# Graph attention over 1,024 nodes: part of each query's edges kept in the query's row and added on GpSimd, the rest summed on TensorE, with a paced stream of projections

## The chip, the cores and the metric

One core of one Trainium2 chip. The time is device microseconds (us) of one execution of the whole program, inputs and outputs in HBM. The kernel before took 2595.01 us, the median of 3 runs (2594.36 to 2597.61).

## The reference, cut to what matters

Sixteen batches of 1,024 nodes with 512 features go through one layer of masked attention with 8 heads of 64, a residual and a layer norm. Everything is float32. The mask `adj` is the same for all batches and heads; it is sparse and uneven, since the chance of an edge falls with both node numbers.

```python
_w = (1.0 + jnp.arange(1024, dtype=jnp.float32)) ** -0.5
_w = _w / _w.mean()
_pij = jnp.clip(0.00390625 * _w[:, None] * _w[None, :], 0.0, 1.0)
adj = (jax.random.uniform(jax.random.fold_in(_gk, 2), (1024, 1024)) < _pij).astype(jnp.float32)
...
q = (x @ Wq + bq).reshape(b, n, H, HD)      # k and v alike
scores = jnp.einsum('bqhd,bkhd->bhqk', q, k) / jnp.sqrt(jnp.float32(HD))
scores = scores + (1.0 - adj)[None, None, :, :] * -1000000000.0
attn = jax.nn.softmax(scores, axis=-1)
out = jnp.einsum('bhqk,bkhd->bqhd', attn, v).reshape(b, n, d)
return _layernorm(x + out @ Wo + bo)
```

`adj` has 4,043 edges among 1,048,576 places. By tiles of 128 queries they are 1404, 588, 440, 377, 360, 311, 290 and 273; 60 queries have no edge, and their softmax is the mean over all keys.

## The kernel before, in words

The kernel works edge by edge. A *block* is 128 edges, one to a partition. `BLOCKS` gives how many blocks each of the eight query tiles has: 11, 6, 4, 4, 3, 3, 3, 3, in all 37 per batch and 592 for the 16 batches. During the lead-in `edges(t)` (line 271) reads the tile's rows of `adj`, finds the keys of each query with rounds of `max` (L286, L288) and writes for each block the list of key rows (`key_row`), of query rows (`query_row`) and a 128x128 matrix of zeros and ones (`sums`) that says which edge belongs to which query. Unused places of a block fetch row 0 and have a zero row in `sums`.

Projections (*fronts*): for each batch and each of its 8 tiles, `front` (line 393) gives 4 TensorE matmuls of 128x512 for q, for k and for v (L377), and a transposition of x two tiles ahead (L359). VectorE adds the biases (L397, L404), and the results go to HBM as rows: `q_rows` (512 wide) and `kv_rows` (1,024 wide, k and v side by side), each held for two batches. Row N of `kv_rows` has key zero and the mean of v, for a query without edges. Squares on ScalarE (L388) and sums on VectorE (L389) feed a guard: where the norms of q and k are too large for an exponential without a maximum, or the edges don't fit their blocks, a flag sends the work to `tile_general`.

Each block then goes through these operations:

- `gather`, 8 steps ahead: two indirect DMAs on GpSimd's queue, the query rows (L501, 128x512) and the key-value rows (L506, 128x1024)
- `scores`: on VectorE the product of query and key (L515, 128x512) and its sum by head (L517)
- `exponentials`: on ScalarE 128x8 (L522), written behind the weighted values in the tile `pv`
- `weigh`: v times the exponentials on VectorE (L533, 128x512). In batch 0 every second block, and in batch 15 two of three, are weighed on ScalarE with 8 operations (L529)
- `add_up`: two TensorE matmuls with `sums` as weights (L545, L546; each float32 matmul is two instructions) add the edges up by query, into PSUM, over the blocks of the tile

After the last block of a tile, `normalise` divides by the sum of exponentials on VectorE (L553, L554, L557), TensorE transposes (L566), and the tile is *done*. `finish` multiplies with Wo (L377, `po`), adds y, which is x loaded once more with the bias added on GpSimd (L461), and does the layer norm: L468, L471, L472, L474 on VectorE, L477 to L479 on GpSimd, L482 on ScalarE, and the store.

The order is written out by hand, one step `n` of the loop at line 594 per block, 34 lead-in steps ahead of block 0. A step issues the gather of block n+8, the weighing of block n+1, the scores of n+2, whatever earlier steps have put off to this one (`later`, collected in `plan`), the exponentials of n+2 and the sums of block n. Then TensorE gets units of projections and finishes until the step's `credit` is used up. `share`, the credit per step, is set once per batch from what is to be done (`PRODUCT` 0.86 a matmul, `TRANSPOSE` 0.44). Within a batch the fronts of the next batch come first, and the finishes only when no fronts are left. Each engine runs its instructions in this order. Tiles with a `tag` are rings of `bufs` buffers: who writes the next one waits until the last reader of the old one is through.

Of the kernel before, what the change touches and what calls it, by code (L numbers as in the profile page):

```python
# [9 lines left out]
F32 = mybir.dt.float32  # L10
# [123 lines left out]
def kernel(  # L134
# [29 lines left out]

    nc = tc.nc
# [7 lines left out]
    assert N == 1024 and D == 512 and HD == 64  # L173
    NB = sum(BLOCKS)
    first = [sum(BLOCKS[:t]) for t in range(NT)]

# [15 lines left out]
    with ExitStack() as main:  # L192
# [6 lines left out]
        def fill_psum(name):  # L199
            return psum.tile([P, HALF], F32, tag="fill", name=name, bufs=4)  # L200
# [7 lines left out]

        place = one.tile([P, max(BLOCKS) * P], F32, name="place")
        nc.gpsimd.iota(place, pattern=[[1, max(BLOCKS) * P]], base=1, channel_multiplier=0, allow_small_or_imprecise_dtypes=True)  # L210
# [15 lines left out]
        sums = one.tile([P, NB, P], F32, name="sums")  # L226
        key_row = one.tile([P, NB], I32, name="key_row")
        query_row = one.tile([P, NB], I32, name="query_row")
# [3 lines left out]
        kv_rows = [dram.tile([N + 1, 2 * D], F32, name=f"kv_rows_{i}") for i in range(2)]  # L232
        q_rows = [dram.tile([N, D], F32, name=f"q_rows_{i}") for i in range(2)]
        zero = one.tile([1, D], F32, name="zero")
        nc.gpsimd.memset(zero, 0.0)
        for i in range(2):
            nc.scalar.dma_start(kv_rows[i][N:N + 1, 0:D], zero)
# [7 lines left out]
        def bias_setup():  # L245
# [7 lines left out]
            bvb = work.tile([P, NPAIR, P], F32, tag="y", name="bvb", bufs=7)  # L253
# [17 lines left out]
        def edges(t):  # L271
            nb, J = BLOCKS[t], DEGREE[t]
# [5 lines left out]
            deg, end, lim, lone = (st[:, i:i + 1] for i in range(4))  # L278
            kl = small.tile([P, J + 2], F32, tag=f"kl{J}", name=f"kl_{t}", bufs=2)
            yield  # L280
# [4 lines left out]
            for r in range(J // 8):  # L285
# [7 lines left out]
            nc.vector.tensor_scalar(lone, kl[:, 0:1], 0.0, N + 1.0, op0=OP.is_le, op1=OP.mult)  # L293
            nc.vector.tensor_tensor(kl[:, 0:1], kl[:, 0:1], lone, op=OP.add)
            nc.vector.tensor_scalar(deg, deg, 1.0, None, op0=OP.max)
# [4 lines left out]
            nc.vector.tensor_copy(kl[:, J:J + 1], po[:, 0:1])  # L300
            nc.vector.tensor_copy(kl[:, J + 1:J + 2], query[:, t:t + 1])
            nc.vector.tensor_tensor(end, kl[:, J:J + 1], deg, op=OP.add)
            nc.vector.tensor_scalar(lim, end, -float(nb * P), 0.0, op0=OP.add, op1=OP.max)
            nc.vector.scalar_tensor_tensor(
                check[:, NT + t:NT + t + 1], deg, -float(J), lim, op0=OP.add, op1=OP.max
# [4 lines left out]
            nc.vector.tensor_scalar(o, span, kl[:, J:J + 1], None, op0=OP.is_gt)  # L310
# [3 lines left out]
            for i0 in range(0, nb, step):  # L314
# [16 lines left out]
                nc.vector.tensor_scalar(e[:, 1, :], e[:, 1, :], -1.0, 0.0, op0=OP.add, op1=OP.max)  # L331
                nc.vector.tensor_scalar(key_row[:, g0:g0 + n], e[:, 1, :], float(N), None, op0=OP.min)
# [60 lines left out]
        def front(b, t):  # L393

            def out_q(p):
                q = work.tile([P, D], F32, tag="q", name=f"q_{b}_{t}", bufs=2)
                nc.vector.scalar_tensor_tensor(q, p, scale, bq_bc, op0=OP.mult, op1=OP.add)  # L397
                nc.sync.dma_start(q_rows[b % 2][ds(t * P, P), :], q)
                later(1, lambda: norm(b, t, 0, q))
# [7 lines left out]
            def out_v(p):  # L407
                kv = KV[b, t]
                XT.pop((b, t))
                nc.scalar.copy(kv[:, D:], p)  # L410
                nc.sync.dma_start(kv_rows[b % 2][ds(t * P, P), :], kv)
                later(1, add_v)
                if t == NT - 1:
                    later(2, mean_v)
# [11 lines left out]
            def mean_pe():  # L426
# [3 lines left out]
                def out():  # L430
                    m = work.tile([1, D], F32, tag="sq", name=f"mean_{b}", bufs=2)
                    nc.scalar.copy(m, p[0:1, :])
                    nc.sync.dma_start(kv_rows[b % 2][N:N + 1, D:], m)
# [23 lines left out]
        def load_y(b, t):  # L457
            Y[b, t] = work.tile([P, D], F32, tag="y", name=f"y_{b}_{t}", bufs=7)
# [35 lines left out]
        KG, QG, PV, SUM = {}, {}, {}, {}  # L494
        blocks = [(b, t, i) for b in range(B) for t in range(NT) for i in range(BLOCKS[t])]

        def gather(n):
            b, t, i = blocks[n]
            g = first[t] + i
            QG[n] = work.tile([P, D], F32, tag="qg", name=f"qg_{n}", bufs=7)  # L500
            nc.gpsimd.indirect_dma_start(  # L501
                out=QG[n], out_offset=None, in_=q_rows[b % 2],
                in_offset=bass.IndirectOffsetOnAxis(ap=query_row[:, g:g + 1], axis=0),
            )
            KG[n] = work.tile([P, 2 * D], F32, tag="kvg", name=f"kvg_{n}", bufs=8)
            nc.gpsimd.indirect_dma_start(  # L506
                out=KG[n], out_offset=None, in_=kv_rows[b % 2],
                in_offset=bass.IndirectOffsetOnAxis(ap=key_row[:, g:g + 1], axis=0),
            )
# [3 lines left out]
        def scores(n):  # L513
            m = QG.pop(n)
            nc.vector.tensor_tensor(m, m, KG[n][:, 0:D], op=OP.mult)  # L515
# [3 lines left out]
        def exponentials(n):  # L519

            PV[n] = work.tile([P, D + HEADS], F32, tag="pv", name=f"pv_{n}", bufs=4)
            nc.scalar.activation(PV[n][:, D:], S.pop(n), AF.Exp)  # L522
# [15 lines left out]

        def add_up(n):
            b, t, i = blocks[n]  # L540
            if i == 0:
# [3 lines left out]
            nc.tensor.matmul(SUM[b, t][:, 0, 0:HD2], m, pv[:, 0:HD2], **kw)  # L545
            nc.tensor.matmul(SUM[b, t][:, 1, 0:HD2 + HEADS], m, pv[:, HD2:], **kw)  # L546
            if i == BLOCKS[t] - 1:
                later(1, lambda: normalise(b, t))

        def normalise(b, t):  # L550
            s = SUM.pop((b, t))
            r = small.tile([P, HEADS], F32, tag="rden", name=f"rden_{b}_{t}", bufs=2)
            nc.vector.tensor_scalar(r, s[:, 1, HD2:HD2 + HEADS], 1.0e-30, None, op0=OP.max)  # L553
            nc.vector.reciprocal(r, r)  # L554
            o = work.tile([P, D], F32, tag="o", name=f"o_{b}_{t}", bufs=2)
            for i in range(2):
                nc.vector.tensor_tensor(  # L557
                    o[:, ts(i, HD2)].rearrange("p (h d) -> p h d", d=HD),
                    s[:, i, 0:HD2].rearrange("p (h d) -> p h d", d=HD),
                    r[:, ds(i * HEADS // 2, HEADS // 2), None].to_broadcast([P, HEADS // 2, HD]), op=OP.mult,  # L560
                )

            def transpose():
# [4 lines left out]
                def out():  # L568
                    OT[b, t] = work.tile([P, D], F32, tag="oT", name=f"oT_{b}_{t}", bufs=7)
# [8 lines left out]
        done = []  # L578
# [6 lines left out]
        with tc.manual_schedule():  # L585
            gathered = 0
            fronts, finishing = [], []
            front_batches = 0
# [3 lines left out]
            fronts += transpose_x(0, 0) + transpose_x(0, 1)  # L592
            n = -LEAD_IN
            while n < total or plan or urgent or done or finishing:
                now[0] = n

                if front_batches < B and front_batches <= max(n // NB, 0) + 1:
                    fronts += [u for t in range(NT) for u in front(front_batches, t)]
                    front_batches += 1
# [5 lines left out]
                while gathered < min(n + AHEAD + 1, total) and blocks[gathered][0] in set_up:  # L605
                    gather(gathered)
                    gathered += 1
# [88 lines left out]
```

## Time and profile before

| | |
|---|---|
| median of the runs | 2595.01 us |
| the profiled execution | 2595.89 us, its span 2594.1 us |
| PE (TensorE) busy | 2477.6 us, 96% |
| DVE (VectorE) busy | 1968.2 us, 76% |
| POOL (GpSimd) busy | 1499.0 us, 58% |
| ACT (ScalarE) busy | 698.7 us, 27% |
| DMA | 678.01 MB, mean 261 GB/s |
| mean granted TensorE clock | 0.982 |

Times in the trace count from the first instruction of the profiled execution. "Busy" is time in which at least one instruction of the engine runs; consecutive instructions of one engine overlap at their ends, so the distance between starts says better than the duration what one costs. Ends of matmuls are modelled, their starts are measured. PEld is TensorE's loading of weights. Idle time of an engine is put down to what ended it.

### The profile page before, as it was taken

What the parts mean: (1) busy time and instruction counts of PE and PEld (TensorE: products, weight loads), DVE (VectorE), ACT (ScalarE), POOL (GpSimd) and SP (SyncE); (2) the same over time, 40 slices, a digit from 0 to 9 for tenths busy, and PEclk for the clock granted to TensorE, in tenths of its full rate; (3) what the DMA queues carried; (4) which work ended last, traced back from release to release, by engine and by line L of the source; (5) the groups of instructions that cost most, each with busy time, mean ns of one, the idle gap of its engine ahead of it and who ended that gap; (6) DMA issues with size and microseconds to landing.
All of it is one profiled execution on the core that took longest, in us unless ns stands there. A gap on an engine that the chain in (4) does not pass through costs nothing.

```text
span 2594.1 us, 26742 instructions
## 1 busy us (share of the span) xinstructions
PE 2477.6 (96%) x7659; PEld 1352.6 (52%) x7659; DVE 1968.2 (76%) x3613; ACT 698.7 (27%) x1764; POOL 1499.0 (58%) x1717
## 2 busy tenths in 40 slices
PE   6988999999999999999999999999999999999967
PEld 3545555555555555555555555555555555555534
DVE  5668778778778877877777777877877777787766
ACT  1345322222222222222222222222222222222254
POOL 0156755647566574756647465564756557475675
PEclk9989999999999999999999999999999999999978
DMA  4368887887879788787878878787887978878785
GB/s 154 110 243 290 270 291 247 286 270 271 283 237 307 254 291 267 257 292 244 301 253 292 271 235 306 244 294 256 277 288 233 309 251 287 264 256 287 230 277 179
DMA packets 228679, 678.01 MB, mean 261 GB/s; under 512 B 29454, under 2 KB 29466, under 8 KB 228524
## 3 DMA queue, kind: packets, MB, share of 16 engines
q0 software_dynamic: 132608, 465.64, 56.3%
q1 hardware_dynamic: 93344, 205.60, 21.2%
q10 hardware_dynamic: 2572, 4.99, 0.5%
q8 instruction: 62, 1.02, 0.2%
q14 instruction: 93, 0.76, 0.1%
HBM read 541.86 MB, written 134.25 MB: 261 GB/s over the span
## 4 chain that ended last, share of the span: by engine, by line
PE 68%; POOL 11%; DVE 10%; issue 7%; ACT 2%; DMA 1%; ACTq 0%; POOLq 0%; another core or an unknown queue 0%; SPq 0%; DVEq 0%
PE pv L377 16%; PE pk L377 15%; PE pq L377 15%; PE sum L546 7%; PE sum L545 7%; POOL kvg L506 4%; PE po L377 4%; POOL y L461 3%; POOL qg L501 2%; DVE y L468 2%; DVE stats L471 2%; PE pxT L359 2%; PE poT L566 2%; DVE qg L515 1%; DVE pv L533 1%
## 5 line engine op out<-in xcount | busy, mean ns | idle before, releaser
L501 POOL DMA_INDIRECT qg<-q_rows,query_row x592 | 586.9, 991 | 588.1 <-DVE s L517 453.7
L506 POOL DMA_INDIRECT kvg<-kv_rows,key_row x592 | 588.7, 994 | 195.2 <-issue 182.9
L533 DVE TENSOR_TENSOR pv<-kvg,pv 128x512 f32<-128x512 f32 x550 | 394.3, 717 | 223.1 <-ACT pv L522 146.8
L377 PE MATMUL pq<-wq,xT 128*128 128x512 f32 x1024 | 482.7, 597 | 14.7 <-ACT xT L363 13.2
L377 PE MATMUL pk<-wk,xT 128*128 128x512 f32 x1024 | 488.9, 598 | 7.1 <-ACT xT L363 7.1
L377 PE MATMUL pv<-wv,xT 128*128 128x512 f32 x1024 | 479.1, 593 | 0.0
L377 PE MATMUL po<-wo,oT 128*128 128x512 f32 x1024 | 473.9, 602 | 0.0
L515 DVE TENSOR_TENSOR qg<-qg,kvg 128x512 f32<-128x512 f32 x592 | 432.6, 731 | 0.3 <-issue 0.3
L517 DVE TENSOR_REDUCE s<-qg 128x8 f32<-128x512 f32 x592 | 406.1, 686 | 20.5
L545 PE MATMUL sum<-pv,sums 128*128 128x256 f32 x1184 | 361.6, 387 | 46.4 <-DVE pv L533 33.8
L545 PEld LDWEIGHTS sum<-pv,sums 128*128 128x128 f32 x1184 | 222.2, 192 | 326.5 <-issue 239.0
L522 ACT ACTIVATE pv<-s 128x8 f32<-128x8 f32 x592 | 124.1, 210 | 929.2 <-DVE s L517 626.5
L546 PE MATMUL sum<-pv,sums 128*128 128x264 f32 x1184 | 366.6, 392 | 4.6 <-ACT pv L529 2.3
L377 PEld LDWEIGHTS pk<-wk,xT 128*128 128x128 f32 x1024 | 194.3, 192 | 193.3 <-issue 175.7
L377 PEld LDWEIGHTS po<-wo,oT 128*128 128x128 f32 x1024 | 192.9, 194 | 182.6 <-issue 173.3
L377 PEld LDWEIGHTS pv<-wv,xT 128*128 128x128 f32 x1024 | 190.5, 191 | 167.0 <-issue 158.4
L377 PEld LDWEIGHTS pq<-wq,xT 128*128 128x128 f32 x1024 | 187.1, 192 | 159.2 <-issue 135.0
L546 PEld LDWEIGHTS sum<-pv,sums 128*128 128x128 f32 x1184 | 226.2, 192 | 41.6 <-ACT pv L529 6.4
L461 POOL TENSOR_TENSOR y<-y,bo_bc 128x512 f32<-128x512 f32 x128 | 163.4, 1277 | 141.5 <-ACT pv L522 74.7
L468 DVE TENSOR_TENSOR y<-po,y 128x512 f32<-128x512 f32 x128 | 88.0, 688 | 151.5 <-POOL y L461 139.4
L404 DVE TENSOR_TENSOR kv<-pk,bk_bc 128x512 f32<-128x512 f32 x128 | 88.2, 689 | 115.8 <-PE pk L377 87.2
L389 DVE TENSOR_REDUCE nrm<-sq 128x8 f32<-128x512 f32 x256 | 172.9, 676 | 1.4 <-ACT sq L388 1.4
(98 smaller groups left out, 1664.8 us busy)
## 6 DMA issues: line engine op xcount, KB each, us to landing
kv_rows<-kv SPq DMA_DIRECT2D x128, 512.0 KB
x<-in_x_dram SPq DMA_DIRECT2D x128, 256.0 KB
q_rows<-q SPq DMA_DIRECT2D x128, 256.0 KB
y<-in_x_dram SPq DMA_DIRECT2D x128, 256.0 KB
out_dram<-y SPq DMA_DIRECT2D x128, 256.0 KB
qg<-q_rows,query_row POOLq DMA_INDIRECT x592
kvg<-kv_rows,key_row POOLq DMA_INDIRECT x592
a<-in_adj_dram SPq DMA_DIRECT2D x8, 512.0 KB
```

The costliest lines, as they stand in the source:

```text
L377: nc.tensor.matmul(p, lhs()[:, ts(c, P)], w[:, c, :], start=(c == 0), stop=(c == NPAIR - 1))
L389: later(1, lambda: nc.vector.tensor_reduce(NRM[b][:, i, t, :], sq.rearrange("p (h d) -> p h d", d=HD), axis=AX.X, op=OP.add))
L461: later(2, lambda: nc.gpsimd.tensor_tensor(Y[b, t], Y[b, t], bo_bc, op=OP.add))
L468: nc.vector.tensor_tensor(y, p, y, op=OP.add)
L501: nc.gpsimd.indirect_dma_start(out=QG[n], out_offset=None, in_=q_rows[b % 2], in_offset=bass.IndirectOffsetOnAxis(ap=query_row[:, g:g + 1] ...
L506: nc.gpsimd.indirect_dma_start(out=KG[n], out_offset=None, in_=kv_rows[b % 2], in_offset=bass.IndirectOffsetOnAxis(ap=key_row[:, g:g + 1], ...
L515: nc.vector.tensor_tensor(m, m, KG[n][:, 0:D], op=OP.mult)
L517: nc.vector.tensor_reduce(S[n], m.rearrange("p (h d) -> p h d", d=HD), axis=AX.X, op=OP.add)
L522: nc.scalar.activation(PV[n][:, D:], S.pop(n), AF.Exp)
L533: nc.vector.tensor_tensor(pv[:, 0:D].rearrange("p (h d) -> p h d", d=HD), v[:, D:].rearrange("p (h d) -> p h d", d=HD), pv[:, D:, None].to ...
L545: nc.tensor.matmul(SUM[b, t][:, 0, 0:HD2], m, pv[:, 0:HD2], **kw)
L546: nc.tensor.matmul(SUM[b, t][:, 1, 0:HD2 + HEADS], m, pv[:, HD2:], **kw)
```

## The change

Some edges of each query no longer go into mixed blocks. `OWN` gives, per tile, a number of blocks in the queries' order: in own block i, partition p holds the i-th edge of the tile's query p. Such a block needs no query gather, since the tile's rows of q, loaded once per tile by a plain DMA on SP's queue (`QT`), serve all of them. It needs no `sums` matrix either: its weighted values and exponentials are added to those of the tile's first own block by one GpSimd operation of 128x520 (`add_own`). Only the edges beyond these go into mixed blocks (`BLOCKS`), which are summed on TensorE as before; the normalisation adds both parts.

- Per batch there are 21 own and 15 mixed blocks, 36 steps instead of 37, 576 in all. Own blocks come first in each tile.
- A place without an edge gets the row number 65536. The key-value gather now has a bounds check and skips such rows, for own and mixed blocks; for own blocks a bias of -1e9 (`absent`) takes their exponentials to zero. The 8 gather buffers are filled with zeros once, at the start, by GpSimd, so that what a skipped row leaves there is finite.
- `normalise` moves from `later(1)` of the last block into the next tile's first step, and is: an addition of 8 columns, an addition of 512 columns with PSUM, the reciprocal, and one product in place.
- PSUM: one buffer pair for sums instead of two, and 6 instead of 4 for everything else (`fill`).
- Order: all fronts stand in one list, and `share` is set so that at the end of a batch the fronts are 2 batches and 14 steps (`EARLY`) ahead. A step with sums pays `SUM` = 0.87 for them from its credit. A finish starts when a tile is done and y was asked for, at least two steps after the one before, ahead of fronts. `q_rows` and `kv_rows` are kept for three batches.
- `edges` writes the own rows and `absent`, and counts the other edges without them: some ten small VectorE operations more per tile, one step more.

The diff, cut to its core:

```diff
+OWN = (7, 3, 3, 1, 1, 2, 2, 2)
-BLOCKS = (11, 6, 4, 4, 3, 3, 3, 3)
+BLOCKS = (5, 2, 1, 2, 2, 1, 1, 1)
+KG_BUFS, QG_BUFS, QT_BUFS, PV_BUFS = 8, 5, 3, 4
+NO_ROW = 65536.0
+ROWS = 3
+EARLY = 14
+SUM = 0.87
...
-            return psum.tile([P, HALF], F32, tag="fill", name=name, bufs=4)
+            return psum.tile([P, HALF], F32, tag="fill", name=name, bufs=6)
...
+            rows, missing = kr[:, 0:K], absent[:, own[t]:own[t] + K]
+            nc.vector.tensor_scalar(rows, kl[:, 0:K], -1.0, float(N), op0=OP.add, op1=OP.min)
+            nc.vector.tensor_scalar(missing, rows, 0.0, None, op0=OP.is_lt)
+            yield
+            nc.vector.scalar_tensor_tensor(
+                key_row[:, NS + own[t]:NS + own[t] + K], missing, NO_ROW, rows, op0=OP.mult, op1=OP.max
+            )
+            nc.vector.tensor_scalar(missing, missing, -NEG, None, op0=OP.mult)
+            nc.vector.tensor_scalar(deg, deg, -float(K), 0.0, op0=OP.add, op1=OP.max)
...
         def gather(n):
             b, t, i = blocks[n]
-            g = first[t] + i
-            QG[n] = work.tile([P, D], F32, tag="qg", name=f"qg_{n}", bufs=7)
-            nc.gpsimd.indirect_dma_start(
-                out=QG[n], out_offset=None, in_=q_rows[b % 2],
...
+            if i == 0:
+                QT[b, t] = work.tile([P, D], F32, tag="qt", name=f"qt_{b}_{t}", bufs=QT_BUFS)
+                nc.sync.dma_start(QT[b, t], q_rows[b % ROWS][ds(t * P, P), :])
+            if i < OWN[t]:
+                g = NS + own[t] + i
+            else:
+                g = first[t] + i - OWN[t]
+                QG[n] = work.tile([P, D], F32, tag="qg", name=f"qg_{n}", bufs=QG_BUFS)
+                nc.gpsimd.indirect_dma_start(
+                    out=QG[n], out_offset=None, in_=q_rows[b % ROWS],
...
             nc.gpsimd.indirect_dma_start(
-                out=QG[n], out_offset=None, in_=q_rows[b % 2],
...
+                out=KG[n], out_offset=None, in_=kv_rows[b % ROWS],
+                in_offset=bass.IndirectOffsetOnAxis(ap=key_row[:, g:g + 1], axis=0),
+                bounds_check=N, oob_is_err=False,
             )
...
-            PV[n] = work.tile([P, D + HEADS], F32, tag="pv", name=f"pv_{n}", bufs=4)
-            nc.scalar.activation(PV[n][:, D:], S.pop(n), AF.Exp)
+            b, t, i = blocks[n]
+            if i == 0:
+                PV[n] = work.tile([P, D + HEADS], F32, tag="pv0", name=f"pv_{n}", bufs=2)
+            else:
+                PV[n] = work.tile([P, D + HEADS], F32, tag="pv", name=f"pv_{n}", bufs=PV_BUFS)
+            bias = absent[:, own[t] + i:own[t] + i + 1] if i < OWN[t] else 0.0
+            nc.scalar.activation(PV[n][:, D:], S.pop(n), AF.Exp, bias=bias)
...
+        def add_own(n):
+            b, t, i = blocks[n]
+            pv = PV.pop(n)
+            if i == 0:
+                PV[b, t] = pv
+            else:
+                nc.gpsimd.tensor_tensor(PV[b, t], PV[b, t], pv, op=OP.add)
...
-                SUM[b, t] = psum.tile([P, 2, HALF], F32, tag="sum", name=f"sum_{b}_{t}", bufs=2)
+                PSUM[b, t] = psum.tile([P, 2, HALF], F32, tag="sum", name=f"sum_{b}_{t}", bufs=1)
...
+            nc.vector.tensor_tensor(r, s[:, 1, HD2:HD2 + HEADS], pv[:, D:], op=OP.add)
+            nc.vector.tensor_tensor(
+                o.rearrange("p (a d) -> p a d", a=2), s[:, :, 0:HD2], pv[:, 0:D].rearrange("p (a d) -> p a d", a=2),
+                op=OP.add,
+            )
             nc.vector.reciprocal(r, r)
...
+            o8 = o.rearrange("p (h d) -> p h d", d=HD)
+            nc.vector.tensor_tensor(o8, o8, r[:, :, None].to_broadcast([P, HEADS, HD]), op=OP.mult)
...
+        for i in range(KG_BUFS):
+            nc.gpsimd.memset(work.tile([P, 2 * D], F32, tag="kvg", name=f"kvg_first_{i}", bufs=KG_BUFS), 0.0)
...
-                    tiles = len(done) + (NT if n + NB < total else NT + 2)
-                    share = (sum(u[0] for u in fronts) + tiles * NPAIR * PRODUCT) / NB
...
+                    left = sum(u[0] for u in fronts)
+                    goal = fronts_time - (n // NB + 2 + EARLY / NB) * batch_time
+                    share = (max(0.0, left - goal) + NT * NPAIR * PRODUCT + NS * SUM) / NB
...
+                if 1 <= n <= total and (n == total or blocks[n][2] == 0):
+                    normalise(*blocks[n - 1][:2])
...
+                credit += share
+                if 0 <= n < total and blocks[n][2] >= OWN[blocks[n][1]]:
                     add_up(n)
-                for tile_done in done[:2]:
+                    credit -= SUM
+                elif 0 <= n < total:
+                    add_own(n)
+                for tile_done in done[:1]:
...
-                    if not fronts and not finishing and done and n > loaded.get(done[0], n):
+                    if not finishing and done and n > loaded.get(done[0], n) and n > last_finish + 1:
                         finishing = finish(*done.pop(0))
+                        last_finish = n
```

More of the change, by code (lines that the diff above doesn't have):

```diff
@@ L172 @@
     scale = 1.0 / HD ** 0.5
-    assert N == 1024 and D == 512 and HD == 64
-    NB = sum(BLOCKS)
+    assert N == 1024 and D == 512 and HD == 64 and max(BLOCKS) <= NT
+    NS = sum(BLOCKS)
+    NB = NS + sum(OWN)
     first = [sum(BLOCKS[:t]) for t in range(NT)]
+    own = [sum(OWN[:t]) for t in range(NT)]
     const = ctx.enter_context(tc.tile_pool(name="const", bufs=1))
@@ L277, in edges @@
             st = small.tile([P, 4], F32, name="est")
-            deg, end, lim, lone = (st[:, i:i + 1] for i in range(4))
+            deg, end, lim, off = (st[:, i:i + 1] for i in range(4))
             kl = small.tile([P, J + 2], F32, tag=f"kl{J}", name=f"kl_{t}", bufs=2)
+            kr = small.tile([P, max(OWN)], F32, tag="kr", name=f"kr_{t}", bufs=2)
             yield
@@ L591 @@
                 load_x(0, t)
-            fronts += transpose_x(0, 0) + transpose_x(0, 1)
             n = -LEAD_IN
```

110 lines of the change are left out of this document (54 added, 56 removed).

## Prediction

> **What bounds the kernel now.** I read first the windows of the trace, cut where block 0 of a batch is summed: lead-in, batch 0, batch 1, the twelve batches 2 to 13 in one, batch 14, and batch 15 with the tail. Columns: length, busy microseconds (instructions) of PE, its weight loads, DVE, ACT, POOL, then the granted clock, the DMA share and GB/s.
>
> ```profile
> 0.00:162.40 162.40, 136.76 (x401) 67.10 (x402) 92.67 (x172) 47.69 (x84) 32.57 (x36) 0.98 0.44 155
> 162.40:309.50 147.10, 127.28 (x423) 73.60 (x422) 118.42 (x247) 73.40 (x232) 96.67 (x97) 0.92 0.79 269
> 309.50:460.00 150.50, 150.50 (x471) 82.90 (x470) 117.47 (x215) 34.80 (x83) 85.81 (x97) 1.00 0.81 268
> 460.00:2306.10 1846.10, 1819.17 (x5641) 996.66 (x5640) 1436.03 (x2593) 439.00 (x1032) 1102.84 (x1273) 1.00 0.82 272
> 2306.10:2458.50 152.40, 150.31 (x462) 82.05 (x462) 118.10 (x219) 35.37 (x84) 92.61 (x107) 1.00 0.80 266
> 2458.50:2594.10 135.60, 93.61 (x267) 50.27 (x266) 85.51 (x171) 68.40 (x250) 88.55 (x112) 0.81 0.68 227
> ```
>
> The fourth window holds twelve batches of 37 blocks by the count of L545's matmuls in it, 888 = 12 x 37 x 2 (PE and weight loads of that line alone):
>
> ```profile
> 460.00:2306.10 1846.10, 266.70 (x888) 166.82 (x888) 1.00 0.82 272
> ```
>
> A middle batch takes 1846.1/12 = 153.8 us. PE is busy 151.6 of them at full clock, DVE 119.7, POOL 91.9, ACT 36.6. So PE sets the pace, and DVE has 34 us of slack. Busy PE ends are modelled, so I checked by starts, in the timeline of batch 6 (PE):
>
> ```profile
> 1201.16 0.59 PE L545 MATMUL sum<-pv,sums 128*128 128x256 f32 x2
> 1201.59 0.61 PE L546 MATMUL sum<-pv,sums 128*128 128x264 f32 x2
> 1202.04 3.60 PE L377 MATMUL po<-wo,oT 128*128 128x512 f32 x8
> 1205.47 0.59 PE L545 MATMUL sum<-pv,sums 128*128 128x256 f32 x2
> ```
>
> One block's sums occupy PE from 1201.16 to 1202.04, 0.88 us. The eight entries that follow are four products, 3.43 us, 0.86 each. There is no gap: in this stage PE time removed is span removed, until DVE becomes the limit. What DVE does per block and per tile, from the same stretch:
>
> ```profile
> 1201.45 0.68 DVE L533 TENSOR_TENSOR pv<-kvg,pv 128x512 f32<-128x512 f32 x1
> 1202.05 0.68 DVE L515 TENSOR_TENSOR qg<-qg,kvg 128x512 f32<-128x512 f32 x1
> 1202.77 0.69 DVE L517 TENSOR_REDUCE s<-qg 128x8 f32<-128x512 f32 x1
> 1203.37 0.15 DVE L553 TENSOR_SCALAR rden<-sum 128x8 f32<-128x8 f32 x1
> 1203.56 0.20 DVE L554 RECIPROCAL rden<-rden 128x8 f32<-128x8 f32 x1
> 1203.80 0.76 DVE L557 TENSOR_TENSOR o<-sum,rden 128x256 f32<-128x256 f32 x2
> 1204.47 0.68 DVE L468 TENSOR_TENSOR y<-po,y 128x512 f32<-128x512 f32 x1
> ```
>
> Start to start: a block's three operations take 1.92 us (1201.45 to 1203.37), a tile's normalisation 1.10 (1203.37 to 1204.47). Last, the waits (microseconds in all, times, longest), as it matters who can hold up DVE once it has no slack:
>
> ```profile
> POOL qg L501 <- DVE s L517: 453.7, 225, 5.3
> DVE pv L533 <- ACT pv L522: 146.8, 68, 5.9
> DVE y L468 <- POOL y L461: 139.4, 64, 5.4
> ```
>
> GpSimd waits for DVE to free gather buffers, not the reverse. DVE's own waits of 147 and 139 us, together 18 us a batch, lie in its 34 us of slack today.
>
> **The change part by part, for a middle batch.** *Sums.* 37 blocks become 36, of which 15 (BLOCKS) are summed on TensorE; 22 times 0.88 = 19.4 us of PE go. PE needs 151.6 - 19.4 = 132.2; with today's 2.2 us of gaps (153.8 - 151.6) the floor is **134.4**.
>
> *GpSimd.* An own block gathers no queries, so 74 gathers become 36 + 15 = 51. In return come 21 - 8 = 13 additions of 128x520 (the first block of each tile only gives its buffer).
>
> ```profile
> 1203.87 0.94 POOL L506 DMA_INDIRECT kvg<-kv_rows,key_row  x1 [0.30 <-issue]
> 1205.11 0.95 POOL L501 DMA_INDIRECT qg<-q_rows,query_row  x1 [0.30 <-issue]
> L461 POOL TENSOR_TENSOR y<-y,bo_bc 128x512 f32<-128x512 f32 x128 | 163.4, 1277 | 141.5 <-ACT pv L522 74.7 <-DMA y<-in_x_dram 40.4 <-issue 24.1
> ```
>
> A gather takes 1.24 us with its 0.30 issue, an addition 1.28 x 520/512 = 1.30. GpSimd today: 91.9 + 74 x 0.30 = 114.1; then 114.1 - 23 x 1.24 + 13 x 1.30 = **102.5**, under PE's. The bounds check on the key gather stands in no row. Below, 505 of 4,608 rows a batch are missing and skipped (counted from adj), 11% of 0.94, -0.1 each; above, the slowest key gather of this trace:
>
> ```profile
> L506 POOL DMA_INDIRECT kvg<-kv_rows,key_row x592: 937/943/1967, 137.9 to 2555.6; - x198
> L515 DVE TENSOR_TENSOR qg<-qg,kvg x592: 676/684/2156, 153.7 to 2569.1; 128x512 f32<-128x512 f32 x198
> L533 DVE TENSOR_TENSOR pv<-kvg,pv x550: 678/682/2366, 158.4 to 2572.9; 128x512 f32<-128x512 f32 x184
> ```
>
> (minimum/median/maximum ns). That is +1.02 each, 36.7 a batch, GpSimd at 139. I take zero, as the median is 6 ns from the minimum: the price hardly varies. If it isn't zero, its cover is the 32 us by which PE exceeds GpSimd.
>
> *What queues behind the additions.* An addition waits for its block's weighing, and stands on GpSimd behind the gather of step n; behind it stand y's bias additions, the rstd steps and the next gathers. The exponentials of block n+2 reuse one of four pv buffers, so ACT now waits for an addition two steps old instead of a matmul: two steps are 7.7 us against 1.24 + 1.24 + 1.30, so nothing. SP gets 128 loads of query tiles, issued eight steps ahead, covered by those steps; the 352 query gathers of the same size go. Rows kept three deep and 14 steps more of projections only bring writes forward. DMA moves less per batch than now (22 query gathers of 256 KB fewer, 8 plain loads more, and the skipped rows); the batch is shorter by about as much, so its share stays near 0.82.
>
> *DVE.* One block less: -1.92. The normalisation becomes an 8-wide addition (0.19, as L553), a 512-wide addition with PSUM (0.60 to 0.72, L533's and L515's pitches), a reciprocal (0.24) and a 512-wide product in place (0.60 to 0.72): 1.63 to 1.87, I take 1.75, so +0.65 x 8 = +5.2. Then the additions on GpSimd cost DVE something, as this stretch shows:
>
> ```profile
> 937.27 2.14 DVE L515 TENSOR_TENSOR qg<-qg,kvg 128x512 f32<-128x512 f32 x1
> 937.57 1.28 POOL L461 TENSOR_TENSOR y<-y,bo_bc 128x512 f32<-128x512 f32 x1
> L515 DVE TENSOR_TENSOR qg<-qg,kvg 128x512 f32<-128x512 f32 x592 | 432.6, 731 | 0.3 <-issue 0.3
> L533 DVE TENSOR_TENSOR pv<-kvg,pv 128x512 f32<-128x512 f32 x550 | 394.3, 717 | 223.1 <-ACT pv L522 146.8 <-ACT kv L410 38.8 <-issue 21.2
> ```
>
> A DVE product of 0.68 us took 2.14, ending 0.56 after a GpSimd addition. L515's mean is 47 ns over its median and L533's 35, so 592 x 0.047 + 550 x 0.035 = 47 us were lost, 0.37 for each of the 128 bias additions. With DVE busy 93% of the batch instead of 78% I scale to 0.44: 13 x 0.44 + 8 x 0.07 = +6.3. The bounds are nothing and, if every addition meets a product, 2.16 - 0.68 = 1.47 each, +19.1. DVE: 119.7 - 1.9 + 5.2 + 6.3 = **129.3**.
>
> The Trainium skill (SBUF — State Buffer, Who interferes with whom) says that a DVE instruction with both inputs in SBUF and a GpSimd instruction that reads SBUF shut each other out for the whole instruction; the trace agrees (2.14 beside 1.28), and by that rule, at its hardest, every addition would shut DVE out for its full 1.30, which makes DVE 123.0 + 13 x 1.30 = 140 instead of 129. The same notes (GPSIMD Engine Reference, Engine selection) would keep element-wise additions off GpSimd, being about half as fast there; the trace agrees (1.28 against 0.69 for L468's shape), and by that rule they would cost DVE 13 x 0.6 = 7.8, against 6.3 of stolen time where they are, so the two placements come out nearly alike.
>
> *Coupling.* PE at 132 and DVE at 129 can't both run full. DVE's plan items of a step need PE's step before, PE's sums need DVE's weighing and, with one sum buffer instead of two, the normalisation of the tile before: neither gets more than a step or two ahead. The eight steps with a normalisation ask DVE for 1.92 + 1.75 and a 36th of the rest, (129.3 - 36 x 1.92 - 14)/36 = 1.28, 4.95 in all; PE has 132.2/36 = 3.67 a step. Of the excess, 8 x (4.95 - 3.67) = 10.2, I let half be absorbed by the step or two of room (chosen, not derived): 134.4 + 5 = **139**. The better pacing (finishes spread over the batch instead of bunched at its end) is in that half.
>
> **The ends.** The lead-in does 33 x 3.45 of projections, of 86 a batch: 1.33 batches, before and after. Batch 0 then did 0.67; now the goal of 2 + 14/36 gives it 1.06, batch 14 only 0.61, batch 15 none as before. Eight fills of 128x1024 are added on GpSimd at the start, beside this idle stretch:
>
> ```profile
> 2.81 0.51 POOL L235 MEMSET zero<- 1x512 f32 x1
> 11.39 2.34 POOL L276 TENSOR_TENSOR codes<-a,place 128x1024 f32<-128x1024 f32 x1 [8.07 <-DMA a<-in_adj_dram]
> ```
>
> at 2 x 0.51 each they just fill its 8.07 us. Lead-in: 162, unchanged. Batch 0: PE +0.39 x 86 - 19.4 = +14, where 20 of 147 us were idle: 152 (147 to 161). Batch 1, for which batch 0 ran ahead: 134. Batch 14: PE near 100, DVE 129 - 9 = 120 and some waits: 124. Batch 15 and tail: GpSimd 12 less, DVE about 10 more, less gathered, while on ACT, which weighs two blocks of three there, this stays:
>
> ```profile
> 2500.48 2.02 ACT L529 ACTIVATE pv<-kvg,pv 128x64 f32<-128x64 f32 x8
> ```
>
> 135.6 becomes 120 (110 to 136). Sum: 162 + 152 + 134 + 12 x 139 + 124 + 120 = 2360 against 2594.1. Around its span the profiled execution had 2595.89 - 2594.1 = 1.8 us more and lay 0.9 over the median 2595.01, so I keep **2360 us**.
>
> **Rivals.** (1) PE stays the sole bound, DVE's waits fall where PE has queued products: 134.4 a batch, 2360 - 12 x 4.6 - 8 = 2297. For it speaks that own blocks ask nothing of PE; against it the 18 us of DVE waits, which then hardly fit. (2) DVE is the bound: the additions come right after a weighing, when DVE starts its next product, and each costs near 1.47. DVE 123.0 + 19.1 = 142, with 5 of waits 147, and 20 more at the ends: 2360 + 12 x 8 + 20 = 2476. For it speaks the 2.14 above; against it that such a meeting was rare, 0.37 on average. The skill's page on SBUF, named above, points this way too. (3) Slower than before: the checked gather is dearer on GpSimd than any row here. 102.5 + 36 d passes 153.8 from d = 1.42, two and a half times 0.94; at d = 2 a batch is 175 and the time about 2360 + 15 x 36 = 2900. Against it: no key gather took over 1.97. (4) The change doesn't do what it says: no batch shorter, because the guard sends the work to the general path. The largest rest of a tile is 254 of 256 rows and 599 of 640, counted from adj, so it can't.
>
> **Chances.** Forecast 0.48, (1) 0.24, (2) 0.20, (3) 0.04, the rest (between (2) and no change) 0.04. The range goes from 2265, under (1) with the ends at their better bounds, to 2490, over (2). A measurement of this kernel can tell about 0.2%, 5 us, from no change: faster 0.95, same 0.01, slower 0.04.
>
> **What would show it.** Right: 240 blocks summed on PE, middle batches near 139, DVE busy over 90% in them, L515's and L533's successors with a mean over 50 ns above the median, PE with gaps that end at DVE. (1) shows as PE without gaps, (2) as PE gaps over 12 us a batch and maxima of 2.1 us by the hundred, (3) as DMA_INDIRECT of kvg near 2 us and DVE waiting for GpSimd. The forecast is wrong if the clock falls below 1.00 in the middle batches, or if DVE waits for a query tile or for DMA.

## The result, and the profile after

The changed kernel takes 2448.0 us, the median of 4 runs (2437.71 to 2456.36), against 2596.31 before: the ratio is 0.942, 95% interval 0.938 to 0.947. That is 148 us less, inside the range on record and 88 us above its 2360. Its profiled execution took 2437.71 us, the shortest of the four, with a span of 2435.9. First the windows of the kernel after, cut where the scores of a batch's first block start on VectorE (lead-in, batch 0, batch 1, batches 2 to 13, batch 14, batch 15 with the tail; columns as in the prediction, from PE to GB/s):

```profile
0.00:146.30 146.30, 126.28 (x350) 59.88 (x351) 89.62 (x169) 42.38 (x69) 29.26 (x33) 1.00 0.42 149
146.30:309.50 163.20, 141.48 (x403) 69.87 (x402) 148.34 (x298) 83.02 (x252) 96.72 (x90) 0.95 0.70 232
309.50:445.60 136.10, 130.27 (x368) 64.89 (x367) 128.96 (x211) 36.01 (x82) 96.38 (x97) 0.97 0.75 252
445.60:2146.10 1700.50, 1614.08 (x4585) 806.82 (x4584) 1602.30 (x2556) 450.01 (x1020) 1150.80 (x1153) 0.98 0.75 251
2146.10:2289.10 143.00, 109.85 (x295) 55.77 (x294) 132.08 (x207) 31.36 (x74) 95.40 (x97) 0.88 0.68 226
2289.10:2435.90 146.80, 82.76 (x190) 41.22 (x189) 96.88 (x170) 70.05 (x250) 91.53 (x100) 0.76 0.52 172
```

A middle batch went from 153.8 to 1700.5/12 = 141.7 us. DVE is busy 133.5 of them (119.7 before), PE 134.5: DVE, which had 34 us of slack, has 8. Cut at the same places, the kernel before had 303.4 us up to batch 1, then 151.9, 1846.1, 152.5 and 140.2. So 145.6 us were won in the middle batches, 15.8 in batch 1 and 9.5 in batch 14, and 6.1 and 6.6 were lost at the beginning and the end. DVE's new time is not work: it runs 213 instructions in a middle batch (2556/12), three fewer than before. The groups of the kernel after that have both inputs in SBUF, the one that reads PSUM (L611), and the two GpSimd operations:

```profile
L582 DVE TENSOR_TENSOR pv<-kvg,pv 128x512 f32<-128x512 f32 x534 | 480.7, 900 | 40.1 <-ACT pv L571 36.8 <-ACT pv L578 2.1 <-issue 0.9
L559 DVE TENSOR_TENSOR qk<-qt,kvg 128x512 f32<-128x512 f32 x336 | 271.8, 809 | 0.0
L617 DVE TENSOR_TENSOR o<-o,rden 128x512 f32<-128x512 f32 x128 | 167.3, 1307 | 4.4
L594 POOL TENSOR_TENSOR pv<-pv,pv 128x520 f32<-128x520 f32 x208 | 269.6, 1296 | 3.2
L492 POOL TENSOR_TENSOR y<-y,bo_bc 128x512 f32<-128x512 f32 x128 | 169.4, 1323 | 110.1 <-DMA y<-in_x_dram 108.0
```

and by tile, with minimum, median and maximum:

```profile
L582 DVE TENSOR_TENSOR pv<-kvg,pv x534: 673/682/3507, 149.2 to 2397.7; 128x512 f32<-128x512 f32 x178
L611 DVE TENSOR_TENSOR o<-sum,pv x128: 679/681/683, 218.3 to 2413.3; 128x512 f32<-128x512 f32 x128
L617 DVE TENSOR_TENSOR o<-o,rden x128: 691/693/2577, 219.2 to 2414.2; 128x512 f32<-128x512 f32 x128
L559 DVE TENSOR_TENSOR qk<-qt,kvg x336: 676/684/2307, 145.6 to 2398.3; 128x512 f32<-128x512 f32 x168
L544 POOL DMA_INDIRECT kvg<-kv_rows,key_row x576: 986/1062/1965, 133.1 to 2377.0; - x192
L539 POOL DMA_INDIRECT qg<-q_rows,query_row x240: 960/1244/1962, 146.8 to 2375.4; - x120
```

The weighings' median is 682 ns as before, but their mean went from 717 to 900, and L617's is 1307 on a median of 693. L611, as long but with one input in PSUM, never strays from 0.68, though 21 of its 128 ran beside a GpSimd addition. How one weighing came to 3.46 us, in the timeline of batch 8:

```profile
1309.81 3.46 DVE L582 TENSOR_TENSOR pv<-kvg,pv 128x512 f32<-128x512 f32 x1
...
1310.20 1.28 POOL L492 TENSOR_TENSOR y<-y,bo_bc 128x512 f32<-128x512 f32 x1
...
1311.43 1.28 POOL L594 TENSOR_TENSOR pv<-pv,pv 128x520 f32<-128x520 f32 x1
```

Two GpSimd additions ran one behind the other, and the product ended 0.56 us after the second. I call this a hold-up. The three groups lost 534 x 0.218 + 336 x 0.125 + 128 x 0.614 = 237 us so.

That VectorE sets the pace shows in the waits of batches 2 to 13 (us in all, times, longest):

```profile
PE sum L603 <- DVE pv L582: 47.7, 12, 5.3
PE poT L622 <- DVE o L617: 36.9, 20, 3.6
DVE y L499 <- POOL y L492: 32.4, 34, 3.8
DVE pv L582 <- ACT pv L571: 23.5, 46, 0.9
```

The first two rows are 84.6 of the 86 us in which PE is idle there. VectorE itself is idle for 98 us, and no row has it wait for an own addition (L594) or for a DMA.

### The profile page after: what moved, and what is told of

Its sections match the earlier page's. It is cut to its first block, busy times and chain, and to the rows that moved or that the text cites. A ratio compares the mean times of both kernels' runs of the same rounds, so it can differ in the third digit from the quotient of the medians.

```text
span 2435.9 us, 23939 instructions
## 1 busy us (share of the span) xinstructions
PE 2204.7 (91%) x6185; PEld 1098.5 (45%) x6185; DVE 2198.2 (90%) x3606; ACT 712.8 (29%) x1746; POOL 1560.1 (64%) x1565
## 4 chain that ended last, share of the span: by engine, by line
DVE 42%; PE 28%; issue 16%; POOL 7%; DMA 4%; ACT 2%; POOLq 0%; ACTq 0%; SPq 0%; DVEq 0%
DVE pv L582 9%; DVE qk L559 9%; PE pv L406 7%; PE pq L406 6%; PE pk L406 6%; DVE s L561 5%; PE po L406 3%; DVE stats L502 3%; POOL kvg L544 3%; DVE y L499 3%; DVE nrm L418 3%; POOL y L492 2%; DVE o L611 2%; PE sum L603 2%; PE sum L604 2%
## 5 line engine op out<-in xcount | busy, mean ns | idle before, releaser
L582 DVE TENSOR_TENSOR pv<-kvg,pv 128x512 f32<-128x512 f32 x534 | 480.7, 900 | 40.1 <-ACT pv L571 36.8
L561 DVE TENSOR_REDUCE s<-qk 128x8 f32<-128x512 f32 x576 | 395.2, 686 | 19.9
L539 POOL DMA_INDIRECT qg<-q_rows,query_row x240 | 277.9, 1158 | 49.3 <-issue 43.7
L571 ACT ACTIVATE pv<-s,absent 128x8 f32<-128x8 f32 x336 | 101.1, 301 | 629.7 <-DVE s L561 514.5
L559 DVE TENSOR_TENSOR qk<-qt,kvg 128x512 f32<-128x512 f32 x336 | 271.8, 809 | 0.0
L594 POOL TENSOR_TENSOR pv<-pv,pv 128x520 f32<-128x520 f32 x208 | 269.6, 1296 | 3.2
L508 POOL TENSOR_TENSOR rstd<-rstd,neg_half 128x1 f32<-128x1 f32 x128 | 108.5, 848 | 208.0 <-DVE rstd L505 199.1
L492 POOL TENSOR_TENSOR y<-y,bo_bc 128x512 f32<-128x512 f32 x128 | 169.4, 1323 | 110.1 <-DMA y<-in_x_dram 108.0
L603 PE MATMUL sum<-pv,sums 128*128 128x256 f32 x480 | 154.4, 405 | 91.1 <-DVE pv L582 58.5
L603 PEld LDWEIGHTS sum<-pv,sums 128*128 128x128 f32 x480 | 92.2, 199 | 210.2 <-issue 99.3
L617 DVE TENSOR_TENSOR o<-o,rden 128x512 f32<-128x512 f32 x128 | 167.3, 1307 | 4.4
```

The costliest lines, as they stand in the source:

```text
L492: later(2, lambda: nc.gpsimd.tensor_tensor(Y[b, t], Y[b, t], bo_bc, op=OP.add))
L539: nc.gpsimd.indirect_dma_start(out=QG[n], out_offset=None, in_=q_rows[b % ROWS], in_offset=bass.IndirectOffsetOnAxis(ap=query_row[:, g:g + ...
L559: nc.vector.tensor_tensor(m, q, KG[n][:, 0:D], op=OP.mult)
L561: nc.vector.tensor_reduce(S[n], m.rearrange("p (h d) -> p h d", d=HD), axis=AX.X, op=OP.add)
L571: nc.scalar.activation(PV[n][:, D:], S.pop(n), AF.Exp, bias=bias)
L582: nc.vector.tensor_tensor(pv[:, 0:D].rearrange("p (h d) -> p h d", d=HD), v[:, D:].rearrange("p (h d) -> p h d", d=HD), pv[:, D:, None].to ...
```

## The experiments

Theory L: the middle batches are paced by VectorE, held up by GpSimd's additions. Its rival P: by the close coupling of TensorE and VectorE, with one sum buffer. All times are medians of 4 runs, beside 2595.67 to 2596.22 us for the kernel before; the column "middle" is a twelfth of the fourth window.

| Run | us | ratio to before (95%) | middle, us | batch 15 and tail, us |
|---|---|---|---|---|
| before | 2596 | 1 | 153.8 | 140.2 |
| after | 2448.0 | 0.942 (0.938-0.947) | 141.7 | 146.8 |
| e1 own additions on VectorE | 2372.2 | 0.914 (0.912-0.915) | 138.3 | 141.4 |
| e2 own additions left out of the result | 2292.2 | 0.884 (0.882-0.886) | 132.2 | 138.9 |
| e3 credit of the last batch | 2432.2 | 0.937 (0.936-0.939) | 142.6 | 133.3 |
| e4 before, new order alone | 2562.2 | 0.987 (0.986-0.989) | 150.4 | 141.3 |
| e5 after, old order | 2484.0 | 0.957 (0.955-0.958) | 146.6 | 138.1 |
| e6 every 4th weighing on ScalarE | 2393.7 | 0.923 (0.921-0.925) | 138.3 | 146.2 |
| e8 = e1 + e3 + e6 | 2326.8 | 0.897 (0.895-0.899) | 136.1 | 124.5 |
| e9 = e8, y's bias on VectorE | 2289.7 | 0.882 (0.881-0.884) | 133.3 | 125.6 |
| e10 = e9 without e6 | 2325.3 | 0.896 (0.895-0.898) | 135.5 | 127.6 |
| e11 one-input GpSimd operation, own additions left out | 2341.7 | 0.902 (0.900-0.905) | 135.4 | 147.2 |
| e12 before, y's bias on VectorE | 2552.5 | 0.983 (0.982-0.985) | 151.6 | 128.5 |

**e1, additions on VectorE.**

```diff
-                nc.gpsimd.tensor_tensor(PV[b, t], PV[b, t], pv, op=OP.add)
+                nc.vector.tensor_tensor(PV[b, t], PV[b, t], pv, op=OP.add)
```

> The changed kernel with its 13 own additions a batch on VectorE instead of GpSimd. Theory L (VectorE sets the pace of the middle batches: 117 us of its own work, 17 in which a GpSimd operation with inputs in SBUF holds up a VectorE product, 8 idle): the additions cost VectorE 13 x 0.60 = 7.8, the hold-ups fall to about 6 (the eight y additions), 117 + 7.8 + 6 + 8 = 139 a batch instead of 142, about 2400 us in all. Theory P (not the hold-ups but the close coupling of TensorE and VectorE with one sum buffer sets the 142): only work is added to VectorE, 148 a batch, about 2530 us.

L: 76 us faster although VectorE does all that GpSimd did. The middle batches came out as L had them (138.3 against 139); the time is 28 us below its 2400, as the stages outside them are 23 us shorter than in the kernel after (712.3 against 735.4). The window of batches 2 to 13, the three groups, and the own additions:

```profile
432.40:2092.40 1660.00, 1599.96 (x4585) 801.54 (x4584) 1576.23 (x2713) 449.37 (x1020) 945.72 (x997) 0.99 0.77 257
L582 DVE TENSOR_TENSOR pv<-kvg,pv 128x512 f32<-128x512 f32 x534 | 392.0, 734 | 21.1 <-ACT pv L571 20.3
L559 DVE TENSOR_TENSOR qk<-qt,kvg 128x512 f32<-128x512 f32 x336 | 239.3, 712 | 0.0
L617 DVE TENSOR_TENSOR o<-o,rden 128x512 f32<-128x512 f32 x128 | 90.6, 708 | 4.4
L594 DVE TENSOR_TENSOR pv<-pv,pv 128x520 f32<-128x520 f32 x208 | 202.1, 971 | 0.0
```

VectorE runs 157 instructions more in these twelve batches and is busy 26 us less. The means of the three groups are nearly back at the medians. The hold-ups that stay, by y's additions on GpSimd, have moved: the own additions take 971 ns on average where nothing holds them up at 691 (e9).

**e2, no additions.**

```diff
-                nc.gpsimd.tensor_tensor(PV[b, t], PV[b, t], pv, op=OP.add)
+                pass
```

> The changed kernel without the own additions: only the first own block of each tile counts, the other 13 own blocks of a batch are gathered, scored and weighed and then dropped. Theory L: VectorE 117 + 6 + 8 = 131, so TensorE takes over with its 132 and 2 of gaps, 134 to 136 a batch, about 2350 us. Theory P: nothing that sets the pace is touched, 142 a batch, 2440 us or more.

```profile
427.10:2014.00 1586.90, 1577.43 (x4584) 793.22 (x4583) 1461.32 (x2557) 450.07 (x1020) 928.40 (x997) 1.00 0.80 269
```

132.2 a batch, PE with 0.8 us of gaps at full clock; the time is 58 us below the expected 2350. P falls: with the same coupling and the same sum buffer the batch runs at TensorE's pace as soon as VectorE has 10 us to spare.

**e3, the last batch.** The goal of the share turns negative for batch 15: 16 - 17.39 batches. "Left minus goal" is then 1.39 batches of projections that don't exist, and the credit 4.45 us per step instead of 1.13.

```diff
-                    share = (max(0.0, left - goal) + NT * NPAIR * PRODUCT + NS * SUM) / NB
+                    share = ((max(0.0, left - goal) if left else 0.0) + NT * NPAIR * PRODUCT + NS * SUM) / NB
```

> The changed kernel with the credit of the last batch computed without the negative goal: 1.13 us of credit per step instead of 4.45, so finishes come one product per step instead of four at once. Theory S (at the end the products of a finish, issued in one lump behind the transposition of the same step, put TensorE and VectorE in turns): batch 15 and the tail fall from 147 us to about 125, 2425 us in all, the middle batches unchanged. Rival (batch 15 is bound by the weighings on ScalarE or by gathers): 147 stays, 2448 us.

The stage fell by 13.5 us, not by 22, so both expectations missed, S by less; with VectorE relieved as well, the stage comes to 125 to 128 (e8 to e10). The times are 15.8 us apart, with intervals that just overlap. What was in the way shows in the chain of waits at the end of the kernel after, one tile's round (start, us, what):

```profile
2393.65 1.21 DVE o L617
2394.90 1.00 PE poT L622 x4
2395.90 4.80 PE po L406 x8
2400.78 0.70 DVE y L499
2401.50 0.70 DVE stats L502
2402.23 0.19 DVE mv L503
2402.53 0.70 DVE qk L559
2403.26 0.69 DVE s L561
2404.02 0.60 DVE o L611
2404.61 0.12 DVE rden L615
2404.76 1.20 DVE o L617
```

TensorE and VectorE take turns, 11.1 us for a tile of three steps, and four products in a lump take 4.8 us, in a stage with a clock of 0.76, instead of the 3.43 of the prediction's timeline. The goal is negative already in batch 14: 16 - 16.39 batches, and a credit for a whole batch of projections where 0.61 is left. They run out early: the last one in the kernel after starts at 2226.74, and in the last 54 us of that batch PE is busy for half the time:

```profile
2235.00:2289.10 54.10, 27.53 (x71) 15.08 (x72) 48.11 (x78) 7.68 (x20) 32.44 (x36) 0.75 0.58 185
```

e3 leaves this as it is, since projections are left there; what it costs was not tried.

**e4 and e5, the order by itself.** e4 is the kernel before with the new order and no own blocks; e5 the changed kernel with the old order. The core of e4, which e5 takes back:

```diff
-                    tiles = len(done) + (NT if n + NB < total else NT + 2)
-                    share = (sum(u[0] for u in fronts) + tiles * NPAIR * PRODUCT) / NB
+                    left = sum(u[0] for u in fronts)
+                    goal = fronts_time - (n // NB + 2 + EARLY / NB) * batch_time
+                    share = (max(0.0, left - goal) + NT * NPAIR * PRODUCT + NB * SUMC) / NB
...
-                    if not fronts and not finishing and done and n > loaded.get(done[0], n):
+                    if not finishing and done and n > loaded.get(done[0], n) and n > last_finish + 1:
```

> The kernel before with the new order alone (one list of projections, 14 steps ahead, finishes two steps apart, rows kept for three batches, sums paid from the credit) and no own blocks. If the gain comes from the sums taken off TensorE, the middle batches stay at 152 to 154 us, and only the ends move: 2570 to 2600 us. If a good part of it comes from the order, the middle batches fall below 150: 2540 us or less.

> The changed kernel with the old order: projections first in each batch, then all finishes, the credit as before the change. On the kernel before, the new order alone was worth 34 us. If order and own blocks simply add up, 2448 + 34 = 2482 us. Theory L says more: with VectorE near its limit a bunch of eight finishes with 1.7 us of VectorE each, next to the hold-ups, can't be hidden: middle batches 146 to 150, 2500 to 2550 us.

e4 came between its two expectations. The order alone gives 34 us, the own blocks alone 2596 - 2484 = 112; together they are 146 of the 148, so in time they add up. e5's middle batches, 146.6, lie where L had them, but its time doesn't. My reading of L, that bunched finishes would cost VectorE more, was wrong: VectorE is busy 130.5 us a batch in e5, less than the 133.5 of the kernel after, and idle for longer. In e4 the middle batches end at 150.4, with PE's busy time equal to the window:

```profile
470.00:2274.50 1804.50, 1804.50 (x5639) 996.11 (x5638) 1446.33 (x2593) 432.24 (x1032) 1132.27 (x1274) 1.00 0.84 278
```

**e6, VectorE relieved otherwise.**

```diff
-            if (b == 0 and n % 2) or (b == B - 1 and n % 3):
+            if (b == 0 and n % 2) or (b == B - 1 and n % 3) or n % 4 == 0:
```

> The changed kernel with every fourth block weighed on ScalarE in all batches (8 operations, 2.02 us, instead of one product on VectorE); additions still on GpSimd. Theory L: VectorE loses 9 x 0.60 of work a batch and the hold-ups of those products, about 7 us in all; 135 a batch, 2355 us. If VectorE isn't what sets the pace, or if ScalarE's longer work delays the exponentials, nothing is gained: 2440 us or more.

54 us faster, as VectorE sets the pace; but 2394 us instead of 2355, and 3.4 a batch instead of 7. The work went: VectorE is busy 5.5 us less a batch, and idle 2.1 more. The hold-ups didn't: the mean of L559 on `qt` rose from 809 to 843 ns, so GpSimd's additions met other products.

**e8 to e10, edits together.** e8 joins e1, e3 and e6. e9 also moves y's bias addition, and e10 is e9 without e6:

```diff
-            later(2, lambda: nc.gpsimd.tensor_tensor(Y[b, t], Y[b, t], bo_bc, op=OP.add))
...
                 nc.vector.tensor_tensor(y, p, y, op=OP.add)
+                nc.vector.tensor_tensor(y, y, bo_bc, op=OP.add)
```

> Three edits at once: own additions on VectorE, every fourth block weighed on ScalarE, credit of the last batch without the negative goal. Theory L: VectorE 117 + 8 + 6 - 5 = 126 with 8 idle, so TensorE's 132 to 134 take over; 12 us less at the end: 2295 to 2315 us. If the edits don't add up, 2350 to 2370 us as with the additions alone.

> As the run with three edits, and the eight bias additions of y on VectorE too, right behind the addition of the product. No GpSimd operation of 512 columns is left. Theory L: VectorE pays 8 x 0.6 = 5 and gets back nearly all of the remaining 6 us of hold-ups: VectorE products keep to 0.68 to 0.70 us on average, the time is the same within 10 us, TensorE sets the pace. If the hold-ups come from something else than these GpSimd operations (gathers, rstd steps), products stay stretched and the time rises by 60 us or more.

> As the last run (own and bias additions on VectorE, credit of the last batch mended), but without the weighings moved to ScalarE in the middle batches. It parts the two ways in which VectorE was relieved. Theory L: VectorE has 124.6 + 9 x 0.6 = 130 of work a batch without hold-ups, TensorE 132; the two are level again, but VectorE's work now has no steps stretched by 1.3 to 2.8 us: 136 a batch, 2325 to 2340 us, between the run with additions on VectorE alone (2372) and the one with everything (2290). If the hold-ups were all that mattered, 133 a batch and 2290 us.

In e9 no GpSimd operation of 512 columns is left, and the hold-ups are gone; gathers and rstd steps, which stay on GpSimd, cause none:

```profile
429.00:2028.50 1599.50, 1578.81 (x4584) 793.13 (x4583) 1500.60 (x2701) 655.97 (x1884) 817.87 (x901) 1.00 0.79 266
L582 DVE TENSOR_TENSOR pv<-kvg,pv 128x512 f32<-128x512 f32 x396 | 271.0, 684 | 31.5 <-ACT pv L571 31.5
L559 DVE TENSOR_TENSOR qk<-qt,kvg 128x512 f32<-128x512 f32 x336 | 230.4, 686 | 0.0
L617 DVE TENSOR_TENSOR o<-o,rden 128x512 f32<-128x512 f32 x128 | 88.6, 692 | 4.4
```

TensorE sets the pace again, at 133.3 a batch. e8 missed its 2295 to 2315 by 12 us, and e9 gained 37 on it where "within 10" was expected. In e8 VectorE also waits for y's addition on GpSimd, 41 us in the middle batches (`DVE y L499 <- POOL y L492`), and in e9 it doesn't; that wait the expectation left out. e10 came where it was expected. e9 is the version that beats both kernels, 6.5% below the kernel after (2289.7 against 2448.0).

**e11, a GpSimd operation with one input.**

```diff
-                nc.gpsimd.tensor_tensor(PV[b, t], PV[b, t], pv, op=OP.add)
+                nc.gpsimd.tensor_scalar(pv, pv, 1.0, None, op0=OP.mult)
```

> The changed kernel with another GpSimd operation in the place of each own addition: one input instead of two, a multiplication by 1.0 of the block's own 128x520 values in place; the own blocks but the first of each tile are so left out of the sum. Beside the run that leaves the additions out (2292 us, 132 a batch) it shows what any GpSimd operation that reads 520 columns costs VectorE. Theory L1 (any read holds up VectorE products for its duration): products keep being stretched, VectorE near 130 busy, 136 to 141 a batch, 2350 to 2440 us. Theory L2 (only two inputs do it): no stretching beyond that of the y additions, 2290 to 2300 us.

```profile
L594 POOL TENSOR_SCALAR pv<-pv 128x520 f32<-128x520 f32 x208 | 338.8, 1629 | 3.7
L582 DVE TENSOR_TENSOR pv<-kvg,pv 128x512 f32<-128x512 f32 x534 | 407.9, 764 | 64.8 <-ACT pv L571 64.4
L559 DVE TENSOR_TENSOR qk<-qt,kvg 128x512 f32<-128x512 f32 x336 | 246.6, 734 | 0.0
L617 DVE TENSOR_TENSOR o<-o,rden 128x512 f32<-128x512 f32 x128 | 98.8, 772 | 4.4
```

The sum over the three groups is 534 x 0.082 + 336 x 0.050 + 128 x 0.079 = 71 us instead of 237, and in e2, with nothing in its place, it is 72 (means 801, 701 and 715). That looks as if one input cost nothing, but the groups moved apart: L582's mean is lower than in e2, L559's and L617's are higher. The trace has products held up by the new operation with no other beside them, such as:

```profile
857.34 1.37 DVE L559 TENSOR_TENSOR qk<-qt,kvg 128x512 f32<-128x512 f32 x1
857.52 1.55 POOL L594 TENSOR_SCALAR pv<-pv 128x520 f32<-128x520 f32 x1
```

In e11, 87 products with both inputs in SBUF took over 0.80 us beside L594 alone and lost 31 us in all, 0.36 each; in the kernel after there were 130 that lost 143 us, 1.10 each. y's additions alone cost 39 us in e11 where they cost 71 in e2, and so the sums come out alike. So a GpSimd operation with one input does hold VectorE up, which L2 denied, but by far less than its duration, which L1 expected. That e11 is 50 us slower than e2 isn't VectorE's work, which is as long in both (1463.9 and 1461.3 us in the middle batches). There VectorE waits for y's addition 77.6 us in e11 and 34.3 in e2, more than the 38 us between the two windows; no run tests whether that is the cause.

**e12, the kernel before.** The edit to y as in e9, nothing else.

> The kernel before with its bias additions of y on VectorE instead of GpSimd. Theory L: hold-ups fall from 3 us a batch to nothing and VectorE gets 5 us of work; both lie in the 34 us that VectorE waits for TensorE, so nothing moves: 2590 to 2600 us. A change of over 10 us would say that hold-ups cost the kernel before something too.

The expectation failed: 43 us faster. Before, with VectorE's waits of 139 us for y's bias addition, PE had 2.2 us of gaps a batch; now that line of the waits is gone and the gaps are (1818.8 - 1808.3)/12 = 0.9:

```profile
454.20:2273.00 1818.80, 1808.30 (x5642) 995.39 (x5641) 1462.86 (x2690) 433.31 (x1032) 1019.98 (x1177) 1.00 0.84 276
```

Middle batches gave 27 us, the last batch and its tail 12. The edit takes away the hold-ups and that wait at once, so how much each cost the kernel before stays open.

## Why the prediction was right, and where it was wrong

*Sums off TensorE: right.* PE's need was put at 132.2 a batch; e2 runs at 132.2, with PE busy 131.5.

*GpSimd not the bound: right.* A batch has 1150.8/12 = 95.9 us of it busy; with 0.30 of issue for each of 51 gathers, as the prediction counts, that is 111, not 102.5, and still well below 141.7. The checked gather takes 1062 ns in the median instead of 943. That isn't all the check, for which I took zero: the query gather, which has none, rose more, to 1244. By the shortest ones (986 against 937) the check is worth about 0.05.

*VectorE's work: slightly over.* The normalisation was put at 1.75 us; in the timeline of batch 8 it takes 1.51 (1303.26 to 1304.77). What 213 instructions a batch would take without hold-ups is about 117 (133.5 less 16.6 of hold-ups, each instruction against the median of its group), where I had 120.

*Hold-ups: the term that failed by size.* I scaled 0.37 us per GpSimd operation to 0.44 and got 6.3 us more a batch. The three groups' 237 us over 336 operations are 0.71. The mistake was to scale a mean of chance meetings. The meetings became more frequent: the kernel before had 44 products of two SBUF inputs over 0.80 us for 128 GpSimd additions, the kernel after 204 for 336, and 28 of these stand beside two additions in a row. A likely reason, not tested, is that an own addition is released by a weighing and runs behind one gather, about when VectorE starts its next products. So VectorE came to 133.5, not 129.3, between the forecast and rival (2), and PE's gaps to 7.2 us a batch, where (2) had named 12. I had also found the additions nearly as dear on VectorE as on GpSimd, 7.8 against 6.3 a batch; e1 has them 3.4 a batch cheaper there.

*Coupling: right number, wrong reason.* 139 against 141.7 looks close, but my 5 us for unequal steps were chosen; e2 shows that coupling costs next to nothing once VectorE has room. The 141.7 are VectorE's 133.5 plus 8 us of idle time.

*The clock.* I had named a clock below 1.00 in the middle batches as a sign of error. It is 0.98 there, with 7.2 us of PE gaps a batch, 0.99 in e1 with 5.0, and 1.00 in e2 and e9 with 0.8 and 1.7. e2's edit touches GpSimd's work alone and the clock rose with it, so I take it for a consequence of the gaps and not for the cause.

*The ends: the step that failed.* Of the 76 us by which the span lies above the forecast, 32 are in the middle batches and 41 in the last two (143.0 + 146.8 against 124 + 120, less 4.6 because the last stage is cut earlier here: 140.2 instead of 135.6 for the kernel before). Batch 14 was put at 124 for having less to project, with VectorE at 120; it took 143 with VectorE busy 132, as some 20 us of hold-ups lay in it. Batch 15 was put at 120, and became slower than before: I took its credit for spread out, where the formula's negative goal lumps the finishes (13.5 us by e3).

*Order and own blocks.* I put the pacing into the chosen half of the coupling, without a price of its own. By e4 and e5 it is 34 to 36 of the 148 us.

## What to carry to other kernels

Work taken from the busiest engine is worth its time only down to the next engine's load, so price what the change does to that engine's *durations* too, by mean against median of each group, and not only to its list of instructions. Moving an element-wise addition to an idle engine can cost the busy one more than doing it: here 208 additions on VectorE, at 0.97 us on average, were 76 us cheaper than on GpSimd. And equal sums over several groups don't show that nothing changed in them (e11). Last, follow a pacing formula to its last iteration by hand, where its terms can change sign.

## What the runs showed of the hardware that was not expected

A VectorE product with both inputs in SBUF whose recorded start lies ahead of a two-input GpSimd operation's can still end after it, and after two of them: 3.46 us instead of 0.68. In the kernel after, 151 products held up by an own addition end 0.55 to 0.57 us after the recorded end of that addition. The product of two SBUF operands is stretched, the sum of PSUM and SBUF is not (683 ns at most, over 128 in the kernel after, 21 of them beside a GpSimd addition). The Trainium skill (SBUF — State Buffer, Who interferes with whom) speaks of any GpSimd instruction that reads SBUF; e11 agrees, as one with a single input of 520 columns held products up too, by 0.36 us each where the two-input addition cost 1.10.
